# Taking every run-ending self-edge out of a graph layer's gathers, with the remaining edges stored end to end in DRAM

## The chip, the cores and the metric

The kernel runs on one core of one Trainium2 chip. The metric is the device time of one execution in microseconds. Before the change three runs took 15,846.22, 15,847.3 and 15,848.97 us; their median, 15,847.3, is the time that the prediction and the result are measured against. A profiled execution is a run of its own and takes a little longer than these.

## The reference

One layer of a graph network with 50,000 nodes and 1,650,000 edges. A node carries 160 numbers: 64 scalars `s` and 32 vectors `v` of three. Every edge takes the 160 numbers of its source node and four numbers of its own (`e0`, and a vector `e1`), makes a message of 160 numbers, and adds it to its destination node.

```python
loop = arange(50000)
src = concatenate([_s, _d, loop]); dst = concatenate([_d, _s, loop])
o = argsort(dst, stable=True); src = src[o]; dst = dst[o]
...
ss, vv = s[src], v[src]
dot = einsum('eui,ei->eu', vv, e1)
out0 = C0 * (ss * e0 @ W1 + dot * INV3 @ W2)
p3 = (ss @ W3)[:, :, None] * e1[:, None, :] * INV3
p4 = einsum('eui,uw->ewi', vv * e0[:, :, None], W4) * INV3
p5 = einsum('eui,uw->ewi', cross(vv, e1[:, None, :]), W5) * INV6
m = concatenate([out0, (C1 * (p3 + p4 + p5)).reshape(-1, 96)], axis=1)
m_agg = segment_sum(m, dst, num_segments=n)
h = concatenate([m_agg_s @ Ws * LIN_S, m_agg_v @ Wv * LIN_V])      # per node
out = layernorm(x + (x + relu(h)))
```

Three facts of it matter here. The edges come sorted by destination, 33 to a node in the mean, so those of one node are a run of neighbours. The list holds one self-edge for each node (source and destination are the same), and since the sort is stable, it is the last of its run; a random edge can be a self-edge too, but seldom. And the message is linear in the source's 160 numbers and in the edge's four, so the sum over edges of (attribute k times x of the source) can be formed first for each node and each of the four k, and the weights applied after it.

## The kernel before, in words

**Units, groups, pairs.** 128 edges are a *unit*, six units a *group* (768 edges), two groups a *pair*. A group's destinations lie in a window of W = 32 nodes that begins at the destination of the group's first edge. `gather` (L288) fetches the source rows of a unit by one indirect DMA of 128 rows of 640 bytes, which GpSimd issues (L292) with a column of the index tile `si`; a pair needs twelve, into one of six buffers `xg`. `spread` (L297) builds on VectorE, for the same pair, the matrix `ha`: for each unit, 128 edges by 4 x 32 columns, holding attribute k of the edge in column (k, node within the window). `group_sums` (L329) multiplies: for each unit a matrix product of `ha` (128 x 128) with the gathered rows (128 x 160), six units added up in PSUM (`ps`, two buffers). The result for a group is `A`, 4 x 32 rows of 160.

**Chunks and blocks.** Four groups are a *chunk*. `turn` (L459) transposes its `A`s on TensorE, `apply_weights` (L476) multiplies by the prepared weights BWa and BWb. A *block* is 128 nodes of the output, 391 in all. `nodes` (L493) loads the block's rows `xt` of x and builds `hot2`, which places the rows of some chunks in the block; `block` (L506) multiplies by it and, with `norm1` to `norm3`, adds x, normalizes, and the result is stored.

**Super-chunks.** Indices and attributes come in for 20 groups (ten pairs) at once: `load` (L235) reads them, `cast` makes floats of the source and destination numbers, `place` (L267) transposes them on TensorE, so that edges lie along the partitions, and writes `si`, the position in the window `rel`, and the attributes `pk`. Over the loop of pairs, the load of the next super-chunk is issued at the first pair of the present one, its cast a pair later and its place three pairs after that. The first position of each window, `baseB`, is read from the destinations once at the start.

**Self-edges taken out of rows.** The first 60 groups (three super-chunks, pairs 0 to 29) are taken from the edge list as it is. All later groups but the last few are cut from *rows* of 787 edges, out of which 19 self-edges are taken, so that 768 are left. 120 rows are a *pack*, one row on each of 120 partitions; there are 17. The generator `pack` (L354) does the work on VectorE: it reads sources, destinations and attributes of the rows (`prs`, `pra`), marks the self-edges, counts them by a running sum (`cum`), collects the four attributes of each (the accumulating products of L419, into `mine`), and closes the gaps by moves of 1, 2, 4, 8 and 16 places under a mask (L431 to L448). At the end three DMAs store the 120 x 768 edges left in DRAM (`sd`, `ad`; L454 and L455), which `load` reads back (L245, L246). What is taken out comes back in `own` and `group_sums`: SP loads for each packed group the 32 rows of x in its window, four times over (`xo`, 80 KB, at an address read into a register, L318 and L324), and VectorE adds `xo` times the taken attributes to `ps` (L343).

**Order.** Work is written out in the order of the pairs: `gather` of a pair, `spread` of the next one, the sums, and then a share of the steps of the pack in progress. The steps of a pack are spread evenly over the pairs until it is needed: the first pack over pairs 1 to about 18, each later one over the 60 pairs that use the pack before it (`when`). A scheduler then sets the final order of each engine's instructions; semaphores carry the dependences. All plain DMAs go through SP's queue, and each of them waits for the eighth DMA before it on that queue, since they share eight semaphores. The same holds for the gathers on GpSimd.

Of the kernel before, what the change touches and what calls it, by code (L numbers as in the profile page):

```python
# [25 lines left out]

# [7 lines left out]
F32 = mybir.dt.float32  # L35
# [29 lines left out]
RP = 120  # L65

# [3 lines left out]
def plan(n_nodes, n_edges):  # L70

    nblk = 125
    assert n_nodes % nblk == 0
    nb = n_nodes // nblk
    again = 9

    per_unit = P * n_nodes / n_edges
    group = max(g for g in range(1, 17)
                if g == 1 or (g + 0.2) * per_unit + 1 + 5 * math.sqrt(g * per_unit * per_unit / P) <= W)

    out = 0
    while out + 1 <= per_unit * group * (1 + 0.03) - 5 * math.sqrt(group * per_unit * per_unit / P + 1 / 6):
        out += 1
    row = group * P + out
    head = min(HEAD, math.ceil(n_edges / (group * P)))
    packed = max(0, (n_edges - head * group * P) // row // SG * SG) if out else 0
    rest = max(0, n_edges - head * group * P - packed * row)
    ngroups = head + packed + math.ceil(rest / (group * P))
    padded = QG * math.ceil(ngroups / QG)
    end = (head + padded - head - packed) * group * P + packed * row  # L90
    units = P * math.ceil(max(math.ceil(n_edges / P) + again - 1, math.ceil(end / P)) / P)
    return nblk, nb, again, group, units, ngroups, row, head, packed
# [3 lines left out]
def tile_gnn_resnorm(ctx: ExitStack, tc: tile.TileContext, x, src, dst, attr, W1, W2, W3, W4, W5, Ws, Wv, out, n_edges):  # L96
    nc = tc.nc
    N = x.shape[0]
    NBLK, NB, GA, G, NU, NG, L, NH, NPK = plan(N, n_edges)
    NCH = math.ceil(NG / QG)  # L100
    NGP = NCH * QG
    K = L - G * P

    def start(g):

        packed = min(max(g - NH, 0), NPK)
        return (g - packed) * G * P + packed * L

# [88 lines left out]
    def near(c):  # L197
        return start(c * QG) * N / n_edges

    step = QG * max(G * P, L) * N / n_edges  # L200
    off = 6 * math.sqrt(n_edges) / 2 * N / n_edges + W
# [10 lines left out]
    with tc.tile_pool(name="once", bufs=1) as once, tc.tile_pool(name="raw", bufs=2) as rawp, \  # L212
            tc.tile_pool(name="idx", bufs=2) as idxp, tc.tile_pool(name="rows", bufs=6) as rowp, \
            tc.tile_pool(name="far", bufs=3) as farp, tc.tile_pool(name="own", bufs=5) as ownp, \
            tc.tile_pool(name="pack", bufs=1) as packp, tc.tile_pool(name="self", bufs=2) as selfp, \
# [4 lines left out]
            tc.tile_pool(name="psM", bufs=2, space=PSUM) as psM:  # L220

        extremes = once.tile([P, 2, NSC], F32, name="extremes")
        baseB = once.tile([P, NGP], F32, name="baseB")
        rowid = once.tile([P, NCH], F32, name="rowid")
        bank = psC.tile([P, 3, P], F32, name="bank")
# [3 lines left out]

        own_eng = ET.Activation if ET.SP in HELP else ET.SP  # L230
        dq = nc.scalar if ET.SP in HELP else nc.sync
# [3 lines left out]
        def load(s):  # L235

            n = (min(NG, (s + 1) * SG) - s * SG) * G
            g0 = s * SG
            ra = rawp.tile([P, P, NK], F32, name="ra")
            if NH <= g0 < NH + NPK:  # L240
                sd, ad = stored[(g0 - NH) // RP]
                e = slice((g0 - NH) % RP * G * P, ((g0 - NH) % RP * G + n) * P)
                rf = rawp.tile([P, 2, P], F32, name="rf")
                for i in range(2):
                    dq.dma_start(rf[:n, i, :], sd[i:i + 1, e].rearrange("o (u p) -> (o u) p", p=P))  # L245
                dq.dma_start(ra[:n].rearrange("u p k -> u (p k)"), ad[e].rearrange("(u p) k -> u (p k)", p=P))  # L246
                return s, n, None, rf, ra
            e = slice(start(g0), start(g0) + n * P)
            ri = rawp.tile([P, 2, P], I32, name="ri")
            dq.dma_start(ri[:n, 0, :], src1[e].rearrange("(u p) o -> u (p o)", p=P))  # L250
            dq.dma_start(ri[:n, 1, :], dst1[e].rearrange("(u p) o -> u (p o)", p=P))
            dq.dma_start(ra[:n].rearrange("u p k -> u (p k)"), attr[e].rearrange("(u p) k -> u (p k)", p=P))
            return s, n, ri, None, ra

        def cast(loaded):
            s, n, ri, rf, ra = loaded
            if rf is None:
                rf = rawp.tile([P, 2, P], F32, name="rf")
                nc.scalar.copy(rf[:n], ri[:n])
            if HELP:  # L260

                ro = rawp.tile([P, P], I32, name="ro")
                nc.scalar.mul(ro[:n], rf[:n, 0, :], 4.0 * D)
                offsets[s] = ro
            return s, n, rf, ra

        def place(cast_):  # L267

            s, n, rf, ra = cast_
            pi = bank[:, 1:3, :]  # L270
            for i in range(2):
                nc.tensor.transpose(pi[:, i, :n], rf[:n, i, :], ident[:n, :n])
            pk = psK.tile([P, NK, P], F32, name="pk")
            for k in range(NK):
                nc.tensor.transpose(pk[:, k, :n], ra[:n, :, k], ident[:n, :n])
            si = idxp.tile([P, P], I32, name="si")
            nc.vector.tensor_copy(si[:, :n], pi[:, 0, :n])
# [4 lines left out]
                float(N - 1), baseB[:, s * SG:s * SG + n // G].unsqueeze(2).to_broadcast([P, n // G, G]),  # L282
# [26 lines left out]
        OWN = 5  # L309

        def own(p):

            s, g, ng = pairs[p]
            if not NH <= g < NH + NPK:
                return
            if p % OWN == 0:
                g1 = min(g + OWN * PG, NH + NPK)
                _, at = nc.values_load_multi_w_load_instructions(  # L318
                    baseO[0:1, g:g1], engines=[own_eng], min_val=0, max_val=(N - W) * 4 * D,
                    skip_runtime_bounds_check_because="an offset of a row of x")  # L320
                places.update(enumerate(at, g))
            xo = ownp.tile([P, PG, D], F32, name="xo")
            for i in range(ng):
                dq.dma_start(xo[:, i, :].bitcast(U8),  # L324
                             xbytes[ds(places.pop(g + i), W * 4 * D)].rearrange("(w f) -> w f", w=W).unsqueeze(0)
                             .to_broadcast([NK, W, 4 * D]))
            owns[p] = xo

        def group_sums(p, rows, ha):  # L329
# [7 lines left out]
            xo = owns.pop(p, None)  # L337
            if xo is None:
                evict(A[:, :ng], ps[:, :ng])
            else:  # L340
                for i in range(ng):
                    r = g0 - NH + i
                    nc.vector.scalar_tensor_tensor(A[:, i], xo[:, i], taken[r // RP][:, r % RP:r % RP + 1], ps[:, i],  # L343
                                                   op0=ALU.mult, op1=ALU.add)
            return A, ng

        owns, stored, taken, places = {}, {}, {}, {}
        halves = ((0, L // 2), (L // 2, L))

        degree = n_edges / N  # L350
        late = 6 * math.sqrt(L) + 2 * degree
        early = -6 * math.sqrt(L)

        def pack(c):  # L354

            r0 = c * RP
            n = min(RP, NPK - r0)
            e0 = start(NH + r0)
            e = slice(e0, e0 + n * L)
            prs = packp.tile([P, 2, L], F32, name="prs")  # L360
            pri = prs.bitcast(I32)
            pra = packp.tile([P, L, NK], F32, name="pra")
            pb = packp.tile([P, 1], I32, name="pb")
            dq.dma_start(pri[:n, 0, :], src1[e].rearrange("(r e) o -> r (e o)", e=L))
            dq.dma_start(pri[:n, 1, :], dst1[e].rearrange("(r e) o -> r (e o)", e=L))
            dq.dma_start(pra[:n].rearrange("r e k -> r (e k)"), attr[e].rearrange("(r e) k -> r (e k)", e=L))
            dq.dma_start(pb[:n], base_d[NH + r0:NH + r0 + n])
            yield
            for _ in range(3):
                yield  # L370
            nc.scalar.copy(prs[:n], pri[:n])
            yield
            marks = psP.tile([P, 512], F32, name="marks")
            m, mi = marks[:n], marks[:n].bitcast(I32)

            cum = packp.tile([P, L + 1], F32, name="cum")
            far = packp.tile([P, L], I32, name="far")
            less = packp.tile([P, L], I32, name="less")
            pbf = packp.tile([P, 2], F32, name="pbf")
            mine = packp.tile([P, 2, NK * W], F32, name="mine")  # L380
            waste = packp.tile([P, L], BF16, name="waste")
            nc.vector.tensor_scalar(pbf[:n, 0:1], pb[:n], float(N - W), None, op0=ALU.min)
            nc.vector.tensor_scalar(pbf[:n, 1:2], pbf[:n, 0:1], -1.0, None, op0=ALU.add)
            nc.vector.memset(mine, 0.0)
            nc.vector.memset(cum[:, 0:1], 0.0)

            for h, (a, e) in enumerate(halves):
                q = slice(0, e - a)
                col = slice(2 * c + h, 2 * c + h + 1)
                nc.scalar.copy(m[:, q], prs[:n, 1, a:e])  # L390
                nc.vector.tensor_tensor(m[:, q], prs[:n, 0, a:e], m[:, q], op=ALU.is_equal)
# [474 lines left out]
```

## Time and profile before

| | |
|---|---|
| three runs, median | 15,847.3 us |
| profiled execution | 15,876.85 us |
| its span | 15,875.1 us |
| granted TensorE clock, mean | 0.669 of full |
| TensorE matmul (PE) | 12,184.3 us busy, 77%, 43,039 instructions |
| TensorE weight load (PEld) | 8,889.9 us, 56% |
| VectorE (DVE) | 6,147.6 us, 39%, 14,632 |
| ScalarE (ACT) | 909.3 us, 6%, 2,081 |
| GpSimd (POOL) | 11,939.1 us, 75%, 12,606 |
| DMA | 1,386.00 MB, mean 87 GB/s |

The page gives for each engine the sum of its instructions' durations. A row of the costliest groups names the source line, the engine, the operation and its tiles (result, arrow, operands), then the count; behind the first bar busy time and the mean of one in ns, behind the second the idle time just ahead of these instructions and what ended it. A row of the timeline has the start in us from the beginning of the span, the busy time, the engine ("SPq" is the queue of DMAs that SP issues), line, operation, count, and in brackets how long the engine had been idle and what released it. "Issue" is idle time in which nothing is waited for that the profile shows. The last part of the page, the chain that ended last, covers less than 1% of this span, so the bound has to be found from groups and timelines.

### The profile page before, as it was taken

The page shows a single profiled execution, that of the slowest core. Times are in us where ns is not written, and L with a number is a line of the kernel's source. Part 1 is how long each engine was busy: PE and PEld are TensorE (multiplying, and loading weights), DVE is VectorE, ACT ScalarE, POOL GpSimd, SP SyncE. Part 2 cuts the span into 40 slices and gives each one's busy share as a digit, 9 for nine tenths or more (in the row PEclk, how much of TensorE's full clock was granted, in tenths as well). Part 3 has the DMA queues.
Part 4 walks back from the last instruction along what each step waited for, and adds up shares of the span by engine and source line. Part 5 has one row for each costly group of instructions (what it writes and reads, how often), then busy time and mean ns, then how long its engine had stood idle before and what let it go on. Part 6 is the DMA issues. An engine that isn't in the chain of part 4 may idle for free. (4 is left out here: it accounts for less than half of the span.)

```text
span 15875.1 us, 127140 instructions
## 1 busy us (share of the span) xinstructions
PE 12184.3 (77%) x43039; PEld 8889.9 (56%) x43040; DVE 6147.6 (39%) x14632; ACT 909.3 (6%) x2081; POOL 11939.1 (75%) x12606
## 2 busy tenths in 40 slices
PE   7677777777777777777777777777777777777777
PEld 5455555555555555555555555555555555555555
DVE  4543344443434343443434343433434343432222
ACT  0000000000000000000000000000000000000000
POOL 7777777777777777777777777777777777777776
PEclk6666666666666666666666666666666666666666
DMA  3333333333333333333333333333333333333332
GB/s 80 90 87 91 83 96 82 95 84 94 83 95 83 90 88 82 95 83 93 84 95 83 95 83 94 84 87 90 84 94 84 95 83 94 83 84 88 83 82 70
DMA packets 1045582, 1386.00 MB, mean 87 GB/s; under 512 B 233195, under 2 KB 818447, under 8 KB 1040753
## 3 DMA queue, kind: packets, MB, share of 16 engines
q0 software_dynamic: 604512, 1032.51, 27.0%
q1 hardware_dynamic: 439801, 344.75, 8.0%
q8 instruction: 338, 5.54, 0.2%
q14 instruction: 323, 2.65, 0.1%
q10 hardware_dynamic: 608, 0.55, 0.0%
HBM read 1307.42 MB, written 69.49 MB: 87 GB/s over the span
## 5 line engine op out<-in xcount | busy, mean ns | idle before, releaser
L292 POOL DMA_INDIRECT xg<-in_x,si x12594 | 11936.8, 948 | 3903.6 <-issue 3657.3
L334 PE MATMUL ps<-xg,ha 128*128 128x160 f32 x25188 | 8819.2, 457 | 3579.1 <-DMA xg<-in_x,si 3535.7
L334 PEld LDWEIGHTS ps<-xg,ha 128*128 128x128 f32 x25188 | 5613.2, 274 | 6208.0 <-DMA xg<-in_x,si 5628.7
L343 DVE SCALAR_TENSOR_TENSOR A<-xo,taken,ps 128x160 f32<-128x160 f32 x2020 | 682.1, 377 | 7006.9 <-PE ps L334 7003.6
L304 DVE TENSOR_TENSOR ha<-hot,pk 128x1536 f32<-128x1536 f32 x1050 | 1828.5, 1742 | 205.3 <-PE ps L334 205.3
L482 PE MATMUL phc<-BWb,at 32*128 32x160 f32 x4200 | 1610.1, 486 | 0.0
L419 DVE SCALAR_TENSOR_TENSOR waste<-marks,pra 120x236 bf16<-120x236 f32 (+45 forms) x2856 | 1492.2, 522 | 44.5
L512 PE MATMUL phb<-hp,hot 128*128 128x160 f32 x4538 | 1325.8, 395 | 0.3 <-DVE hot L502 0.2
L468 PE MATMUL pt<-ident,A 128*128 128x128 f32 (+1 forms) x4198 | 1292.2, 391 | 3.2 <-DVE A L343 0.9
L482 PEld LDWEIGHTS phc<-BWb,at 32*128 32x128 f32 x4200 | 919.3, 272 | 552.6 <-issue 552.6
L482 PE MATMUL phc<-BWa,at 128*128 128x160 f32 x4200 | 1149.4, 372 | 0.0
L512 PEld LDWEIGHTS phb<-hp,hot 128*128 128x128 f32 x4538 | 1082.1, 273 | 4.0 <-ACT at L471 3.5
L482 PEld LDWEIGHTS phc<-BWa,at 128*128 128x128 f32 x4200 | 919.5, 252 | 0.5 <-ACT at L471 0.2
L177 DVE SCALAR_TENSOR_TENSOR y<-phb,xt 128x160 f32<-128x160 f32 x391 | 125.8, 322 | 1969.8 <-PE phb L512 1969.1
L471 ACT COPY at<-pt 128x512 f32<-128x512 f32 (+1 forms) x1050 | 579.8, 579 | 4464.9 <-PE pt L468 4456.2
L468 PEld LDWEIGHTS pt<-ident,A 128*128 128x128 f32 (+1 forms) x4198 | 729.6, 176 | 87.6 <-DVE A L343 16.6
L301 DVE TENSOR_TENSOR hot<-bank,rel 128x384 f32<-128x384 f32 x1050 | 572.5, 546 | 2.4
L486 ACT COPY hp<-phc 128x160 f32<-128x160 f32 x525 | 153.6, 293 | 6019.0 <-PE phc L482 5982.1
L502 DVE TENSOR_TENSOR hot<-bank,rr 128x768 f32<-128x768 f32 (+2 forms) x391 | 357.9, 915 | 0.0
L186 ACT ACTIVATE rstd<-mv,eps_t 128x1 f32<-128x1 f32 x391 | 115.3, 295 | 3938.7 <-DVE mv L181 3902.5
L446 DVE COPY_PREDICATED pra<-marks,pra 120x1572 f32<-120x1572 int32 (+6 forms) x170 | 323.1, 1900 | 0.0
L419 DVE DVE_READ_ACCUMULATOR waste<-marks,pra 120x1 f32 (+1 forms) x2856 | 233.4, 82 | 0.0
(105 smaller groups left out, 1826.1 us busy)
## 6 DMA issues: line engine op xcount, KB each, us to landing
xg<-in_x,si POOLq DMA_INDIRECT x12594
xo<-in_x SPq DMA_DIRECT2D x2020, 80.0 KB
xt<-in_x SPq DMA_DIRECT2D x390, 80.0 KB
out<-o SPq DMA_DIRECT2D x390, 80.0 KB
ra<-ad SPq DMA_DIRECT2D x101, 240.0 KB
pra<-in_attr SPq DMA_DIRECT2D x16, 1475.6 KB
ad<-pra SPq DMA_DIRECT2D x16, 1440.0 KB
rf<-sd SPq DMA_DIRECT2D x202, 60.0 KB
```

What stands on the lines that cost most here:

```text
L292: nc.gpsimd.indirect_dma_start(out=xg[:, j, :], out_offset=None, in_=x, in_offset=bass.IndirectOffsetOnAxis(ap=placed[0][:, u + j:u + j + ...
L301: nc.vector.tensor_tensor(hot[:, :n], slotsP[:, 0:W].unsqueeze(1).to_broadcast([P, n, W]), rel[:, u:u + n].unsqueeze(2).to_broadcast([P, n ...
L304: nc.vector.tensor_tensor(ha[:, :n], hot[:, :n].unsqueeze(2).to_broadcast([P, n, NK, W]), pk[:, :, u:u + n].rearrange("p k u -> p u k").un ...
L334: nc.tensor.matmul(ps[:, j // G, :], ha[:, j].rearrange("p k w -> p (k w)"), xr, start=j % G == 0, stop=j % G == G - 1)
L343: nc.vector.scalar_tensor_tensor(A[:, i], xo[:, i], taken[r // RP][:, r % RP:r % RP + 1], ps[:, i], op0=ALU.mult, op1=ALU.add)
L419: nc.vector.scalar_tensor_tensor(waste[:n, w0:w1], m[:, w0 - a:w1 - a], float(w + 1), pra[:n, w0:w1, k], op0=ALU.is_equal, op1=ALU.mult, a ...
L446: nc.vector.copy_predicated(pra[:n, a:e], mi[:, r].unsqueeze(2).to_broadcast([n, e - a, NK]), pra[:n, a + d:e + d])
L468: nc.tensor.transpose(pt[:f1 - f0, g, :], A[:, i, f0:f1], ident)
L471: evict(at[:, :, :ng].rearrange("f k g w -> f g k w"), pt[:f1 - f0, :ng].rearrange("f g (k w) -> f g k w", w=W))
L482: nc.tensor.matmul(ph[:ng * W], at[:, k, :ng].rearrange("f g w -> f (g w)"), bw[:, k, :], start=i == 0, stop=i == 2 * NK - 1)
L502: nc.vector.tensor_tensor(hot2[:, :len(cs)], slotsP.unsqueeze(1).to_broadcast([P, len(cs), P]), rr[:, :len(cs)].unsqueeze(2).to_broadcast( ...
L512: nc.tensor.matmul(ph[:nb], hot2[:r, i, :nb], hp[:r], start=i == 0, stop=i == len(cs) - 1)
```

## The change

`plan` now counts with all self-edges that end a node's run, not with 19 in a row: a row is 790 edges, there are 2,033 rows in 17 packs, and what is left after the removal fills 2,086 groups instead of 2,099 (12,516 units in place of 12,594). How many edges are left of a row depends on the data, so rows can't be stored at fixed places. They are stored end to end in one DRAM array `edges`, six floats for each edge (source, destination, four attributes); each row's first position follows from its first destination, since one edge is taken for every node passed. `row_table` reads the first destination of all rows by one strided DMA and works out two tables of addresses, one for `edges` and one for the taken attributes, which go to an array `selves`, four floats for each node.

A row is stored by four DMAs, issued by SP, with addresses from registers that are loaded ten at a time (`store`, `put`): the row from its 33rd edge on (18,192 B), the first 32 edges (768 B), and two halves of the taken attributes (256 B each). All tails of a pack are stored first and all heads after them, so that a head overwrites what the row before it left beyond its own end. `load` reads a super-chunk by one DMA from `edges`, once all rows up to its end have been stored. In `pack`, source, destination and attributes stand together in `prow`, and one masked move serves all six. `place` works out the windows from the destinations that it has, by a product with ones on TensorE and some small operations.

The loads `xo` and VectorE's additions in `group_sums` leave; ScalarE copies `ps` to `A` for every pair, as it did for the first 60 groups. The self-edges' messages are added once a block: the new `own(b)` transposes the block's `xt`, multiplies by the weights for two k at a time, multiplies each by the node's taken attribute `sa` (loaded from `selves` in `nodes`) and adds; `block` adds the sum `t`. The gather buffers `xg` go from six to five. The steps of one pack at a time are spread over the pairs until its `due`.

```diff
-            tc.tile_pool(name="idx", bufs=2) as idxp, tc.tile_pool(name="rows", bufs=6) as rowp, \
+            tc.tile_pool(name="idx", bufs=2) as idxp, tc.tile_pool(name="rows", bufs=5) as rowp, \
...
         def load(s):
...
+            if g0 >= NH:
+                p0 = g0 * G * P - EH
+                r6 = rawp.tile([P, P, 2 + NK], F32, name="r6")
+                dq.dma_start(r6[:n].rearrange("u p c -> u (p c)"),
+                             edges[0, p0 * (2 + NK):(p0 + n * P) * (2 + NK)].rearrange("(u q) -> u q", u=n))
+                return s, n, None, r6[:n, :, 0], r6[:n, :, 1], r6[:n, :, 2:]
...
-            if NH <= g0 < NH + NPK:
-                sd, ad = stored[(g0 - NH) // RP]
...
         def place(cast_):
...
+            first = idxp.tile([P, SG], F32, name="first")
+            nc.vector.tensor_scalar(first[:n], starts[:n], df[:, 0:1], None, op0=ALU.mult)
+            nc.tensor.matmul(bank[:, 3, :ng], ones[:n], first[:n, :ng], start=True, stop=True)
+            gs = slice(s * SG, s * SG + ng)
+            nc.vector.tensor_scalar(baseB[:, gs], bank[:, 3, :ng], float(N - 1), None, op0=ALU.min)
...
-        def own(p):
...
             A = sump.tile([P, PG, D], F32, name="A")
-            xo = owns.pop(p, None)
-            if xo is None:
-                evict(A[:, :ng], ps[:, :ng])
-            else:
-                for i in range(ng):
-                    r = g0 - NH + i
-                    nc.vector.scalar_tensor_tensor(A[:, i], xo[:, i], taken[r // RP][:, r % RP:r % RP + 1], ps[:, i],
-                                                   op0=ALU.mult, op1=ALU.add)
+            evict(A[:, :ng], ps[:, :ng])
...
+        def row_table(tmp):
...
+                dq.dma_start(ti[:, :NR], dst[EH:EH + NR * L].rearrange("(o r e) -> o r e", o=1, e=L)[:, :, 0])
...
         def pack(c):
...
+            def begin():
+                T["rows"] = rows = packp.tile([P, L + 1, C], F32, name="prow")
+                nc.scalar.copy(rows[:n, :L, 0], T["pri"][:n, 0, :L])
+                nc.scalar.copy(rows[:n, :, 1], T["pri"][:n, 1, :])
+                nc.scalar.copy(rows[:n, :L, 2:], T["pra"][:n])
...
+                    nc.vector.copy_predicated(rows[:n, a:e], mi[:, r].unsqueeze(2).to_broadcast([n, e - a, C]),
+                                              rows[:n, a + d:e + d])
...
-            for i in range(2):
-                dq.dma_start(sd[i:i + 1].rearrange("o (r e) -> (o r) e", e=G * P), prs[:n, i, :G * P])
-            dq.dma_start(ad.rearrange("(r e) k -> r e k", e=G * P), pra[:n, :G * P])
...
+            def store(head, j):
...
+                _, at = nc.values_load_multi_w_load_instructions(
+                    row_at[0:1, i0:i0 + m], engines=[ET.SP], min_val=0, max_val=row_start(NR - 1)[0][1] * 4 * C,
+                    skip_runtime_bounds_check_because="held within bounds")
+                _, node = nc.values_load_multi_w_load_instructions(
+                    node_at[0:1, i0:i0 + m], engines=[ET.SP], min_val=0, max_val=row_start(NR - 1)[1][1] * 4 * NK,
+                    skip_runtime_bounds_check_because="held within bounds")
+                for i in range(m):
...
+                    e = slice(0, W) if head else slice(W, L)
+                    put(edge_bytes, v, e, C, T["rows"][p:p + 1, e, :])
+                    if r0 + p < real:
...
+                        e = slice(0, W // 2) if head else slice(W // 2, W)
+                        put(self_bytes, v, e, NK, T["mine"][p:p + 1, 0, e, :])
+
+            def put(mem, at, e, width, what):
+                size = (e.stop - e.start) * width * 4
+                dq.dma_start(mem[e.start * width * 4:][ds(at, size)].rearrange("(o f) -> o f", o=1),
+                             what.bitcast(U8).rearrange("p e c -> p (e c)"))
...
+            for head in (False, True):
+                steps += [partial(store, head, j) for j in range(RS)]
...
+            sa = np_.tile([P, NK], F32, name="sa")
+            dq.dma_start(sa[:nb], selves[0, row.start * NK:row.stop * NK].rearrange("(n k) -> n k", k=NK))
...
+        def own(b, xt, sa, hot2):
...
+                nc.tensor.transpose(pt[:f1 - f0, i, :nb], xt[:nb, f0:f1], ident[:nb, :nb])
+                evict(xT[:f1 - f0, i, :nb], pt[:f1 - f0, i, :nb])
+            t = np_.tile([P, D], F32, name="t")
+            for h in range(NK // 2):
+                y = psM.tile([P, 2, D], F32, name="yx", tag="misc")
+                ks = slice(2 * h, 2 * h + 2)
+                nc.tensor.matmul(y[:nb], xT[:, 0, :nb], BWa[:, ks, :], start=True, stop=False)
+                nc.tensor.matmul(y[:nb], xT[:D - P, 1, :nb], BWb[:, ks, :], start=False, stop=True)
...
+                        nc.vector.scalar_tensor_tensor(t[:nb], y[:nb, i], sa[:nb, k:k + 1], t[:nb],
+                                                       op0=ALU.mult, op1=ALU.add)
...
+            nc.vector.tensor_tensor(ph[:nb], ph[:nb], t[:nb], op=ALU.add)
             return norm1(np_, ph[:nb], xt[:nb], nb)
```

## The prediction

> **What bounds the kernel now.** I read the page's busy shares first, then its costliest groups, then GpSimd's timeline.
>
> ```profile
> PE 12184.3 (77%) x43039; PEld 8889.9 (56%) x43040; DVE 6147.6 (39%) x14632; ACT 909.3 (6%) x2081; POOL 11939.1 (75%) x12606
> ...
> L292 POOL DMA_INDIRECT xg<-in_x,si x12594 | 11936.8, 948 | 3903.6 <-issue 3657.3
> L334 PE MATMUL ps<-xg,ha 128*128 128x160 f32 x25188 | 8819.2, 457 | 3579.1 <-DMA xg<-in_x,si 3535.7
> ```
>
> ```profile
> 470.82 0.95 POOL L292 DMA_INDIRECT xg<-in_x,si  x1 [0.30 <-issue]
> 472.07 0.95 POOL L292 DMA_INDIRECT xg<-in_x,si  x1 [0.30 <-issue]
> 489.16 0.95 POOL L292 DMA_INDIRECT xg<-in_x,si  x1 [16.14 <-DVE si L277]
> ```
>
> GpSimd, not TensorE, sets the pace: TensorE's idle time is a wait for gathers, GpSimd's is almost only "issue". A gather takes 0.95 us and 0.30 of issue: one each 1.25 us, 15.02 us for a pair of groups (twelve). 12,594 x 1.2513 = 15,759 of the span's 15,875; the rest is the start (18.7), the end (33) and some 65 us of stalls. The largest stall, 16.1 us, is the third line: the first gather of pair 30, the first to use packed rows, waits for its indices. So there is little to win but gathers, and a lot to lose by anything that makes indices, or a free gather buffer, late.
>
> Why that stall exists is in the timelines of VectorE and of SP's queue:
>
> ```profile
> 370.46 1.75 DVE L304 TENSOR_TENSOR ha<-hot,pk 128x1536 f32<-128x1536 f32 x1 [6.10 <-PE ps L334]
> ...
> 464.46 1.81 DVE L446 COPY_PREDICATED pra<-marks,pra 120x1512 f32<-120x1512 int32 x1
> ```
>
> ```profile
> 464.19 1.20 SPq L454 DMA_DIRECT2D sd<-prs  x2
> 466.30 0.32 SPq L455 DMA_DIRECT2D ad<-pra  x1
> ...
> 476.68 0.81 SPq L245 DMA_DIRECT2D rf<-sd  x2
> ```
>
> VectorE ends the first block of rows only at 466 us, three DMAs store it, and the loads of super-chunk 3 follow. What comes between 466 us and those loads is on the path.
>
> **Prices on SP.** Per instruction, ns min/median/max:
>
> ```profile
> L324 SPq MOVE xo<-in_x x2020: 29/38/38, 39.1 to 15629.0; - x184
> L324 SPq DMA_DIRECT2D xo<-in_x x2020: 539/562/1667, 39.2 to 15629.0; - x184
> L318 SPq TENSOR_LOAD <-baseO x202: 1138/2244/2619, 37.9 to 15566.0; - x101
> L498 SPq DMA_DIRECT2D xt<-in_x x391: 328/359/495, 20.8 to 15835.6; - x196
> ```
>
> ```profile
> 6019.05 1.24 SPq L324 DMA_DIRECT2D xo<-in_x  x2
> ```
>
> A DMA at a fixed address holds SP for 0.36 us, one at an address from a register for 0.56, and two of these with a register move between them take 1.24, so 0.68 apart. A load of ten registers has two sizes in the trace (1.29 and 2.37) and a mean of 1.84.
>
> **What the Trainium skill says.** "DMA: Bandwidth & Descriptors", Rules for kernel authors: transfers under 64 KB are mostly overhead and should be coalesced. The stores added here are 18,192, 768 and 256 B; no run shows such a store yet. Same page, Anatomy of one DMA: about 2 us are fixed per DMA. The trace agrees: its semaphore events put an xt load's last increment 2.1 us (median) after its issue. Same page, Why a DMA increments its semaphore by 16 and not by 1: the number of DMA engines follows from the outermost dimension of the access, so a store from one partition may sit on one engine; no row of this trace is of that kind. "TensorE: Matmul & The Clock Gate", Part 1: activity releases the half clock. The trace fits: clock 0.67 while it waits for gathers.
>
> **The change, part by part.**
>
> *Gathers.* 2,086 groups instead of 2,099: 12,516 gathers, 78 fewer, x 1.2513 = 98 us gained. This part is certain; the built program holds that many.
>
> *Self messages.* Gone: 2,020 loads xo of 80 KB, 202 register loads on SP, 2,020 DVE adds (682 us). New: a copy of A on ACT for each pair (423 ns each in the 40 such copies of before, x 1,043 = 441 us; ACT is 6% busy), and for 391 blocks two transposes, four 320-column matmuls, four DVE products at about 0.38 us and an add at 0.32 (720 us of VectorE, 61% idle). TensorE: a 160-column pass advances 0.2 us at full, 0.37 at half clock in the timeline, so 4 to 7.4 us a block, 1.6 to 2.9 ms in all. Its 3.5 ms of waiting for gathers cover it, and more activity brings more full clock. I cost these at nothing; were TensorE's cover gone, the shortfall would be below 1 ms.
>
> *Start.* The first place now stands on VectorE behind two or three operations on a 1x2040 table, whose strided load comes first on SP: 10 to 15 us later, I take 12.
>
> *The stores.* Each block of 120 rows now leaves as one DMA per row for the tail (18,192 B), one for the head (768 B) and two of 256 B for the self attributes: 480 DMAs, almost all at addresses from registers, with 48 loads of ten registers. They replace three. In the built program the tails have one register operation each, the heads none, and every DMA waits for the one eight back, which at 2 to 4 us of landing is done by then. Price: 0.36 (fixed address) and 0.56 (128 rows from a register) bound one such DMA; a single row needs fewer descriptors, the address still comes from a register, so I take 0.48. With 0.045 of gap, and 0.075 more where there is a register operation: 0.60 for a tail, 0.525 for a head. Sum: 240 x 0.60 + 240 x 0.525 + 48 x (1.84 + 0.11) = 144 + 126 + 94 = 364 us. At the fixed-address price (0.48 and 0.405) it is 306, at xo's (0.68 and 0.60) 402.
>
> *First block.* VectorE: in the built order the product for pair 26 (370.5 in the timeline, plus 12) is followed by 84 collects where 37 stood, the messages of three blocks, then the shifts. The last message waits for TensorE's pair 25 (413), then 22 short collects, then 49 us of shifts (eight steps of 5.3, two of 3.4, as before: a 6-wide copy replaces a 4-wide and two): 413 + 3 + 20 + 49 + 12 = 497. All 480 stores are queued on SP ahead of the load for super-chunk 3: 497 + 364, and 9 for load, transposes and indices = 870. Gathers for pair 30 could start at 473 + 12 = 485. Stall 385 in place of 16: **+369**.
>
> *Later blocks.* 60 pairs apart. The last shift stands after the product for pair 113 (then 173, ...), which VectorE reaches 1 to 2 pairs ahead of its gathers, so stores start near pair 112.5. In 15 pairs (225 us) SP is given 369 us of work (5 for the xt, sa and out among them). Behind them wait the loads xt, the next super-chunk and, through the row buffer of which there is one, ACT's three copies of the next block, which stand after the copy of A for pair 129. ACT blocked there holds the two PSUM buffers, so the products of pair 132 stop, and with five gather buffers so does the gather of pair 137. That leaves 24.5 pairs = 368 us, less 13 (landing 2, ACT 5, TensorE 6): 355. Over by 14, and about 12 for xt and TensorE to catch up: 26 us, x 15 blocks = **+390**. The second block has 22 pairs: 369 - 317 + 12 = **+64**.
>
> Sum against the profiled execution (15,876.9; span 15,875.1): 15,877 - 98 + 12 + 369 + 64 + 390 = 16,614. The runs' median, 15,847.3, lies 30 lower: **16,580 us**.
>
> **Rivals.**
> *Cheap stores* (fixed-address price, 306 us for a block): the later blocks fit in 355 us and nothing stalls there; the first still does, by 327 - 16 = 311. 15,847 - 98 + 12 + 311 = 16,070. For it: a single row is less than xt's 128. Against it: xo's 0.2 us extra, which I lay on the register.
> *Dear stores* (xo's price, 402 us): first block +407, second +102, later (407 - 355 + 12) x 15 = 960: 17,230. The same lies near if all tails go through one DMA engine: in the burst of ad<-pra a 12,288 B packet took 0.72 us, so 18,192 B take up to 1.06, ten in each 16 us beside a gather's 0.34 each 1.25: 66% and 27%, near full. Gathers wait for the one eight back, 10 us; the trace shows 2.6 us of landing, and some 2 us of stall behind the 1.4 MB loads.
> *TensorE becomes the bound*, were its clock not released: some hundred us more, within the range.
> *Not slower*: the stores go out as fast as registers are moved. Then 98 - 12 = 86 us of gain must cover the first block, so 480 stores with their register loads must take under 81 us, 0.17 each. The register loads alone take 94 in the rows above, so this also needs them hidden behind VectorE's work; then 15,760.
>
> **From cases to numbers.** Likeliest case 0.40 (own range 16,350 to 16,850), cheap 0.25, dear or one DMA engine 0.25, TensorE 0.05, not slower 0.05. The ends are the two prices with their errors: 16,000 to 17,300. What a measurement here can tell from no change is 0.2%, 32 us: faster 0.03, same 0.02, slower 0.95.
>
> **What would show it.** 12,516 gathers at 1.25 us; one POOL stall of 300 to 430 us before pair 30, released by VectorE's si; on SP 8,128 DMAs of L540 with a median of 0.4 to 0.56 us; 15 stalls of equal size, 60 pairs apart, with ACT's copies waiting for stores. A first stall under 100 us would make it wrong, as would gathers of more than 1.25 us each away from stores, or a median under 0.2 us at L540.

## The result and the profile after

The changed kernel takes 16,056.3 us (median of four runs, 16,054.1 to 16,058.6), the kernel before 15,847.5 us in the same series: 208.8 us slower, ratio 1.0132 with a 95% interval of 1.0114 to 1.0149. The forecast was 16,580. The sign was right and the likeliest size was 3.5 times too large. The time lies closest to the rival *Cheap stores* (16,070), and so does the pattern: a stall at the first packed pair and nearly none later.

The page after, engines and costliest groups:

```profile
PE 12359.3 (77%) x47011; PEld 8724.9 (54%) x47012; DVE 6413.6 (40%) x15105; ACT 1574.3 (10%) x3873; POOL 11845.4 (74%) x12530
...
L302 POOL DMA_INDIRECT xg<-in_x,si x12516 | 11841.1, 946 | 4157.0 <-issue 3561.3
L324 PE MATMUL ps<-xg,ha 128*128 128x160 f32 x25032 | 7383.7, 423 | 3146.7 <-DMA xg<-in_x,si 3097.5
```

GpSimd still sets the pace: 12,516 gathers of 0.946 us with 0.30 us of "issue" each. What is new stands in GpSimd's timeline; the rows are starts, busy times, and in brackets the idle time before and its releaser:

```profile
486.08 0.94 POOL L302 DMA_INDIRECT xg<-in_x,si  x1 [0.30 <-issue]
775.38 0.94 POOL L302 DMA_INDIRECT xg<-in_x,si  x1 [288.36 <-DVE si L287]
```

```profile
1492.75 0.94 POOL L302 DMA_INDIRECT xg<-in_x,si  x1 [12.05 <-PE ptx L607]
```

These are all the stalls of more than 2 us beyond the usual 0.30: 288 us at the first packed pair (16 before) and 12 us at pair 77. After pair 100 no gap is 1.5 us longer than usual. Where the 288 us come from is in the timelines of VectorE and of SP's queue:

```profile
495.84 2.67 DVE L504 COPY_PREDICATED prow<-marks,prow 120x2274 f32<-120x2274 int32 x1
...
774.85 0.26 DVE L287 TENSOR_SCALAR si<-bank 128x120 int32<-128x120 f32 x1
```

```profile
763.14 0.23 SPq L540 DMA_DIRECT2D selves<-mine  x1
763.42 0.35 SPq L396 DMA_DIRECT2D pri<-in_dst  x1
763.83 0.40 SPq L398 DMA_DIRECT2D pri<-in_dst  x1
764.27 0.86 SPq L238 DMA_DIRECT2D r<-edges  x2
```

VectorE ends the rows of the first block at 498.5 us, SP has issued the 480 stores by 763.4, the load of super-chunk 3 follows at 764.3, and its indices are there at 775. And this is what a store and a register load cost SP (ns, min/median/max):

```profile
L540 SPq DMA_DIRECT2D edges<-prow x4066: 227/228/16622, 495.2 to 14889.8; - x194
L540 SPq DMA_DIRECT2D selves<-mine x4062: 227/228/325, 450.3 to 14890.1; - x194
```

```profile
L519 SPq TENSOR_LOAD <-ti x408: 957/1862/2773, 498.8 to 14880.1; - x136
```

A DMA of one row holds SP for 0.228 us, with 18,192 or 256 bytes alike, where the prediction took 0.48.

The whole difference, in the prediction's terms: 78 gathers fewer at 1.2513 us, -98; the stall at pair 30, 288.1 - 15.8 = +272; the stall at pair 77, +12; the first gather at 25.0 us instead of 18.7, +6; from the last gather to the end 50.3 us instead of 32.7, +18. Together +210, against 208.8 measured. (The two profiled executions differ by 177.2 us only, since that of before took 29 us more than its median and that of after 2 us less.)

### The profile page after: what moved, and what is told of

Same layout as the page of the kernel before. It is cut to its first block, busy times and chain, and to the rows that moved or that the text cites. A ratio compares the mean times of both kernels' runs of the same rounds, so it can differ in the third digit from the quotient of the medians.

```text
span 16052.3 us, 155475 instructions
## 1 busy us (share of the span) xinstructions
PE 12359.3 (77%) x47011; PEld 8724.9 (54%) x47012; DVE 6413.6 (40%) x15105; ACT 1574.3 (10%) x3873; POOL 11845.4 (74%) x12530
## 4 chain that ended last, share of the span: by engine, by line
POOL 46%; issue 21%; PE 16%; DMA 13%; SPq 3%; DVE 1%; ACT 0%; POOLq 0%; DVEq 0%; ACTq 0%
POOL xg L302 46%; DMA xg<-in_x,si 13%; PE ps L324 7%; PE yx L614 3%; PE yx L613 2%; SPq L540 2%; PE pt L559 2%; PE phb L630 1%; PE phc L573 1%; SPq L522 1%; SPq L519 1%; PE ptx L607 0%; DVE pra L465 0%; DVE prow L504 0%; PE pk L285 0%
## 5 line engine op out<-in xcount | busy, mean ns | idle before, releaser
L324 PE MATMUL ps<-xg,ha 128*128 128x160 f32 x25032 | 7383.7, 423 | 3146.7 <-DMA xg<-in_x,si 3097.5
L324 PEld LDWEIGHTS ps<-xg,ha 128*128 128x128 f32 x25032 | 4989.1, 254 | 5478.5 <-DMA xg<-in_x,si 4913.8
L465 DVE SCALAR_TENSOR_TENSOR pra<-marks,prow 120x236 bf16<-120x236 f32 (+40 forms) x2924 | 1501.6, 514 | 33.1
L327 ACT COPY A<-ps 128x320 f32<-128x320 f32 x1043 | 443.4, 425 | 6528.1 <-PE ps L324 6503.8
L614 PE MATMUL yx<-BWb,xT 32*128 32x320 f32 x1564 | 1000.3, 735 | 1.6 <-ACT xT L608 1.6
L613 PE MATMUL yx<-BWa,xT 128*128 128x320 f32 x1564 | 960.8, 713 | 0.7 <-ACT xT L608 0.7
L559 PE MATMUL pt<-ident,A 128*128 128x128 f32 (+1 forms) x4172 | 918.2, 371 | 42.8 <-DVE t L620 30.2
L630 PE MATMUL phb<-hp,hot 128*128 128x160 f32 x4688 | 892.6, 352 | 0.0
L573 PE MATMUL phc<-BWb,at 32*128 32x160 f32 x4176 | 771.4, 327 | 0.0
L620 DVE SCALAR_TENSOR_TENSOR t<-yx,sa,t 128x160 f32<-128x160 f32 x1173 | 445.0, 379 | 329.1 <-PE yx L614 323.3
```

The lines of the kernel that those rows point to most:

```text
L324: nc.tensor.matmul(ps[:, j // G, :], ha[:, j].rearrange("p k w -> p (k w)"), xr, start=j % G == 0, stop=j % G == G - 1)
L465: nc.vector.scalar_tensor_tensor(T["waste"][:n, w0:w1], T["marks"][:n, w0 - a:w1 - a], float(w + 1), T["rows"][:n, w0:w1, 2 + k], op0=ALU. ...
L559: nc.tensor.transpose(pt[:f1 - f0, g, :], A[:, i, f0:f1], ident)
L573: nc.tensor.matmul(ph[:ng * W], at[:, k, :ng].rearrange("f g w -> f (g w)"), bw[:, k, :], start=i == 0, stop=i == 2 * NK - 1)
L613: nc.tensor.matmul(y[:nb], xT[:, 0, :nb], BWa[:, ks, :], start=True, stop=False)
L614: nc.tensor.matmul(y[:nb], xT[:D - P, 1, :nb], BWb[:, ks, :], start=False, stop=True)
```

## The experiments

Two theories were set against each other first: that the loss is the first block alone, whose stores hold SP while no packed row is ready, and that it is spread over all blocks or over the new work in `own`. Then the price of a store and the limit of the later blocks were tried by themselves.

### More plain groups, 120 and 100 instead of 60

```diff
-HEAD = 60
+HEAD = 120
...
-    rows = math.ceil((n_edges - eh) / row) + 2
+    rows = math.ceil((n_edges - eh) / row) + 3
```

> First theory (the loss is the first block alone: its 480 stores hold SP for 265 us while no packed row is ready): with 120 plain groups instead of 60 the first packed pair is 60, not 30, the first block is due 30 pairs (450 us) later and its stores lie under gathers. Stall at pair 60 under 20 us; 12,528 gathers instead of 12,516, +15 us; 16,056 - 272 + 15 = 15,800, range 15,780 to 15,820. Rival (the loss is spread: own(b) on TensorE and the stores of all blocks slow the gathers): a few us at most are gained, 16,030 or more.

> 100 plain groups: first packed pair 50, 12,522 gathers (+7.5 us). First theory: the last masked move of the first block stands some 8 pairs ahead of the due pair 39, so stores run from pair 31 or 32 to pair 49 or 50 and super-chunk 5 is loaded right after: a stall of 5 to 60 us at pair 50; 15,795 to 15,850. Rival (spread loss): 16,030 or more.

In the first series of four kernels the one before took 19,139 us itself (11 runs, 19,088 to 19,225), and there this kernel took 20,782 us and the one with 100 groups 20,764. TensorE and SP were held up between instructions in the traces of that series: with 120 groups 2,643 us of TensorE's idle time are "issue", and none in the trace of the same kernel in the next series. So nothing is concluded from it; the same kernels ran again.

> The same kernel as e1_head120, since in the first call the kernel before itself took 19,139 us instead of 15,847: there TensorE and SP were held up between instructions, which says nothing on the two theories. With the kernel before near 15,847 us the expectation of e1_head120 stands: first theory 15,780 to 15,820 and no stall over 20 us at pair 60; rival 16,030 or more.

Measured: **15,749.9 us** (15,747.0 to 15,754.2) beside 15,845.9 for the kernel before; ratio 0.9940, interval 0.9926 to 0.9953. No stall at pair 60 or anywhere else over 2 us. Its gathers:

```profile
L302 POOL DMA_INDIRECT xg<-in_x,si x12528 | 11854.2, 946 | 3844.2 <-issue 3583.8
```

The stall of 288 us is gone for 12 gathers more, and so is the one of 12 us; this is 306 us less than the changed kernel and 96 less than the one before. The spread theory falls. The first block's rows are ready at 602.9 us, its stores issued by 874.0 (pair 56.2), and the first packed pair starts on time at 932.4. The result is 30 us below the range: the first stall went whole (288, not the 272 counted), and with it the second, 10 us at the start and the end, and some 10 us of gaps under 2 us.

> 100 plain groups, with the kernel before near 15,847 us: 12,522 gathers, 7.5 us fewer than with 120. With 120, stores ended at pair 56.2, 3.8 pairs before the first packed pair. With 100 they end between pair 47 and 50, super-chunk 5 is needed at pair 50: a stall of 0 to 30 us there, 15,742 to 15,775. Were the stores of the first block still exposed, some hundred us: 15,850 or more.

Measured: 15,846.9 us (12 runs), ratio 0.9999, interval 0.9991 to 1.0008. That misses the range by some 70 us and is what was named for stores still exposed:

```profile
883.06 0.94 POOL L302 DMA_INDIRECT xg<-in_x,si  x1 [97.18 <-DVE si L287]
```

The stores do not begin near pair 31 as expected. VectorE ends the first block's rows at 606.8 us (pair 38), as late as with 120 groups, and from there it takes 276 us to the first gather, as in the changed kernel (498.5 to 775.4: 277). Pair 50 was due at 786. What decides is the distance from the end of the moves to the first packed pair: it has to be 277 us. Why VectorE ends as late here as with 120 groups, though the block is due ten pairs earlier, is not shown.

### The kernel before with 80 plain groups

```diff
-HEAD = 60
+HEAD = 80
```

> The kernel before with 80 plain groups instead of 60, to part what the larger number gives by itself from what it gives to the change: the count of gathers stays 12,594, the first block of rows is needed ten pairs later, and the 16 us stall goes. 15,847 - 16 = 15,831, range 15,822 to 15,842.

Measured: 15,827.4 us, inside the range, ratio 0.9988, interval 0.9981 to 0.9994, and the first packed pair starts with no gap. So the larger number by itself is worth 20 us to the old kernel. The other 77 us of the best version (15,827.4 - 15,749.9) are the change's: 66 gathers fewer than 12,594 are 83 us at 1.2513.

### Stores to fixed addresses

```diff
-                _, at = nc.values_load_multi_w_load_instructions(
-                    row_at[0:1, i0:i0 + m], engines=[ET.SP], min_val=0, max_val=row_start(NR - 1)[0][1] * 4 * C,
...
+                    v = (r0 + p) * 766 * 4 * C
...
+                        v = (EH + (r0 + p) * L) // 33 * 4 * NK
...
-                dq.dma_start(mem[e.start * width * 4:][ds(at, size)].rearrange("(o f) -> o f", o=1),
+                dq.dma_start(mem[e.start * width * 4 + at:e.start * width * 4 + at + size].rearrange("(o f) -> o f", o=1),
```

> All 480 stores of a block go to fixed addresses, and the 48 register loads and the register moves are gone (rows then lie where they do not belong, so wrong edges are summed; the amount of work is the same). First theory: the DMA row stays at 0.23 us, with 0.07 between two that is 0.30 x 480 = 144 us for a block in place of 265; the stall at pair 30 falls from 288 to about 167, the one at pair 77 to nothing: 16,056 - 121 - 12 = 15,923. If a register address is what makes a DMA dearer, the row falls clearly below 0.23. Rival (VectorE's late end, not the stores, sets the stall): it stays within 20 us of 288.

> The same kernel as e3_fixed_addresses, with the kernel before near 15,847 us: a store at a fixed address with no register load. First theory: DMA row 0.23, pitch 0.30, 144 us a block; stall at pair 30 167 us instead of 288, at pair 77 none; 15,923, range 15,900 to 15,950. If the register is what costs, the DMA row falls well below 0.23 and the stall below 140. Rival (VectorE sets the stall): 288 within 20.

Measured, in one run each: 19,222 us in the first series, 15,948.3 later, 108 us less than with registers and inside the range. The row of one DMA and the first packed gather:

```profile
L532 SPq DMA_DIRECT2D edges<-prow x4066: 214/250/819, 502.2 to 14768.8; - x194
```

```profile
671.81 0.94 POOL L302 DMA_INDIRECT xg<-in_x,si  x1 [186.49 <-DVE si L287]
```

The stall falls from 288 to 186 us, though VectorE ends its rows 4 us later (502.2): it is SP's stores that fill it, and the theory that VectorE sets it falls. A DMA at a fixed address is not cheaper than one at a register's: 0.25 us against 0.228. What the registers cost are the loads (87 us in the first block of the changed kernel) and a move or two for each DMA. From the end of the moves the 395 stores that are left take 155 us (85 of the attributes' went out before), 0.39 each on average and not 0.30, so the stall is 19 us longer than forecast.

The packets in the trace show where that comes from. Heads and their attributes follow each other every 0.295 us, as forecast. Each tail is a single packet of 18,192 B that takes 0.68 us, no two of the 2,033 overlap, and the 120 of this block fill 83 of 84 us. SP is held through its wait for the DMA eight places back. For the whole run, and below it for the changed kernel (us in total, times, longest):

```profile
SPq L532 <- DMA edges<-prow: 981.5, 1745, 1.5
```

```profile
SPq L540 <- DMA edges<-prow: 41.2, 88, 1.2
```

With the register work between them the 120 tails of the first block hold 82 us of packets in 141 us, so there SP is seldom held.

### The loads xo at fixed addresses, in the kernel before

```diff
-                             xbytes[ds(places.pop(g + i), W * 4 * D)].rearrange("(w f) -> w f", w=W).unsqueeze(0)
+                             xbytes[23 * (g + i) * 4 * D:(23 * (g + i) + W) * 4 * D].rearrange("(w f) -> w f", w=W).unsqueeze(0)
```

> The kernel before, with the loads xo at fixed addresses near the right ones and no register loads (self-edges then take a wrong node's row in part of the groups; the same bytes and shapes are moved). The prediction laid the 0.20 us that an xo DMA costs over an xt DMA on the register. If so, the row falls from 0.56 to 0.36. The rival, after the stores with a register took 0.23: it is the shape (32 rows laid four times), and the row stays at 0.50 or more. The time: 15,847 within 15 either way, since SP is not on the path there.

Measured, in one run: 15,852.6 us, inside the range, and

```profile
L324 SPq DMA_DIRECT2D xo<-in_x x2020: 536/537/1698, 39.9 to 15604.6; - x184
```

It is 0.537 us without a register and 0.562 with one. Of the 0.20 us that an xo load costs over an xt load, 0.025 at most is the register's. By elimination the rest belongs to the shape, 32 rows laid four times over; another shape of that kind was not tried.

### All stores twice, and the stores of rows twice

```diff
                     put(edge_bytes, v, e, C, T["rows"][p:p + 1, e, :])
+                    dq.dma_start(spare[p:p + 1, e.start * C:e.stop * C], T["rows"][p:p + 1, e, :].rearrange("p e c -> p (e c)"))
...
                         put(self_bytes, v, e, NK, T["mine"][p:p + 1, 0, e, :])
+                        dq.dma_start(spare2[p:p + 1, e.start * NK:e.stop * NK], T["mine"][p:p + 1, 0, e, :].rearrange("p e k -> p (e k)"))
```

The second addition is left out where only rows are doubled.

> Each of the 480 stores of a block goes out a second time, to a spare array at a fixed address (nothing else is changed): 960 DMAs, 265 + 480 x 0.30 = 409 us of SP for a block. First theory with the prediction's budget of 355 us for a later block: stall at pair 30 288 + 144 = 432, at the second block 12 + 144 = 156, at each of 15 later ones 409 + 5 - 355 + 12 = 71: 16,056 + 144 + 144 + 1,065 = 17,410. Rival (later blocks have no such limit, SP's work there is hidden anyway): 16,056 + 144 and at most 144 at the second block, 16,200 to 16,345, and no stall over 5 us after pair 100.

> The same kernel as e4_stores_twice, for the same reason. With the kernel before near 15,847 us: first theory 17,410 with a stall of some 71 us at each later block; rival 16,200 to 16,345 and no stall over 5 us after pair 100.

> Only the 240 stores of rows (tails and heads) go out a second time, to a spare array at a fixed address; nothing else is changed. A later block then holds SP for some 421 - 72 = 349 us from its last masked move on (275 before, 421 with all stores twice). Theory of a budget (355 us by the prediction, 421 - 73 + 12 = 360 by the run with all stores twice): no stall, or under 5 us, at the 15 later blocks; first block 288 + 72 = 360, second 50 to 90: 16,056 + 72 + 40 to 80 = 16,168 to 16,210. Rival (every DMA more costs a share, with no threshold): half of what all stores twice cost at the later blocks, 37 x 15 = 550 us more: about 16,740.

Measured, in one run each: all twice 17,492.1 us (22,852 in the first series), 82 above the first theory and over a thousand above its rival; rows twice 16,895.9. GpSimd in the third block, all twice and rows twice:

```profile
2772.73 0.94 POOL L302 DMA_INDIRECT xg<-in_x,si  x1 [57.69 <-PE ps L324]
```

```profile
2640.55 0.94 POOL L302 DMA_INDIRECT xg<-in_x,si  x1 [44.19 <-PE ptx L609]
```

Both are the first gather of pair 137, the pair that the prediction named. The same stall returns at 197, 257 and so on, often with shorter ones two and four pairs earlier. Means of the third to the sixteenth block, from the end of the last masked move to the last store, with SP's other DMAs among them:

| | SP's stores, us | stall per block, us | stores less 343 us |
|---|---|---|---|
| the changed kernel | 276.5 | 0 | below 0 |
| rows twice | 388.7 | 44.6 | 45.7 |
| all twice | 421.5 | 78.4 | 78.5 |

343 comes from the prediction: a later block's stall is its stores less 355 us of room, plus 12 to catch up. Both runs over the limit fit that in the mean, and between them 33 us more of stores cost 34 us more of stall. Single blocks scatter (35 to 72 us with rows twice, 58 to 103 with all twice), and no run of this kind lies between 277 and 389 us, so whether the stall begins at 343 or with a jump at 355 is not shown.

Rows twice missed its number (16,190 for the theory) and lies nearer to the rival's 16,740: the 240 DMAs more took 112 us of SP, 0.47 each, not the 0.30 expected, so this run was over the limit too. Most of the excess is in the tails again: in the third block 240 of them, one packet at a time, take 230 us where 120 took 148. A rival without a limit would have one price for a microsecond of stores, but the first 112 us more cost 45 and the next 33 cost 34. Counted by DMAs (240 more cost 45 us, 480 cost 78) the means do not exclude it; for the limit speak the waits below, which end with the stores.

The way the stall takes is only in part the one predicted. In the third block with all stores twice, TensorE stops first, on the load xt that waits behind the stores on SP:

```profile
2751.74 0.48 PE L611 MATMUL ptx<-ident,xt 128*128 128x128 f32 x1 [87.19 <-DMA xt<-in_x]
```

In the same block with rows twice, ScalarE stops first, as predicted: behind the copy of A for pair 129, at its copy into the row buffer.

```profile
2609.90 2.91 ACT L406 COPY prow<-pra 120x3160 f32<-120x3160 f32 x1 [69.95 <-DMA spare<-prow]
```

TensorE stops 6 us after it, for xt again. Both waits end with the stores, and no run parts the one from the other.

### Without the self-edges' messages

```diff
         def own(b, xt, sa, hot2):
...
-                nc.tensor.matmul(y[:nb], xT[:, 0, :nb], BWa[:, ks, :], start=True, stop=False)
-                nc.tensor.matmul(y[:nb], xT[:D - P, 1, :nb], BWb[:, ks, :], start=False, stop=True)
...
+            return xt, sa, hot2
...
-            nc.vector.tensor_tensor(ph[:nb], ph[:nb], t[:nb], op=ALU.add)
```

> The changed kernel without own(b) and without the addition in block: the self-edges' messages are left out (transposes, four products and five VectorE operations for each of 391 blocks). The loads of xt and sa and all stores stay. First theory: TensorE's work there is covered; the stall at pair 30 stays at 288 within 10, the one at pair 77 (TensorE waiting for xt) goes, and the end is some 15 us shorter: 16,056 - 12 - 15 = 16,029, range 16,010 to 16,050. Rival (own(b)'s 1.96 ms of TensorE are on the path in part): below 15,950.

Measured, in one run: 16,051.2 us, a microsecond outside the range, 5 less than the changed kernel:

```profile
PE 11489.3 (72%) x43101; PEld 8546.1 (53%) x43102; DVE 5737.2 (36%) x13150; ACT 1393.9 (9%) x3091; POOL 11846.1 (74%) x12530
```

```profile
788.64 0.94 POOL L302 DMA_INDIRECT xg<-in_x,si  x1 [302.70 <-DVE si L287]
```

TensorE has 870 us less to do and VectorE 676, and no time comes of it: that work is covered. The end is 22 us shorter (last gather to end 27.9). The two stalls did not do as expected. The first is 14 us longer, not within 10 of 288, because VectorE ends the rows at 512.0 instead of 498.5: the order of its instructions is a different one here. The stall at pair 77 did not go but moved to pair 80, again 12 us, and is now a wait for the load of the next super-chunk behind the stores (stores end at 1541.8, the gather starts at 1552.5).

This run also bounds what the 343 us mean. In every second block from the fourth on, the last store leaves 362 us after the last masked move (58 to 91 us of it SP's wait for a result to send), and no gather is late. TensorE does not read xt here, and ScalarE's copies into the row buffer stand six pairs later in these blocks (in the fourth, behind the copy of A for pair 195, not 189). So the limit belongs to the order of the work that waits behind the stores, not to the stores.

## Why the prediction was right and wrong

**The bound and the gathers: right.** 12,516 gathers came at 1.25 us; nothing between stalls moved. Of the other signs named beforehand, the first stall (300 to 430 us) and the median of a store (0.4 to 0.56 us) came in lower, and the 15 equal stalls did not come.

**Self messages at nothing: right**, by the run without them. What the prediction left out is the end, where nothing covers `own` of the last blocks: 18 us.

**Start: half.** It is +6 us, not +12.

**The price of a store: the step that failed.** The prediction bounded a DMA by 0.36 us (fixed address, 128 rows) and 0.56 (address from a register), laid the difference on the register and took 0.48. Both bounds came from DMAs of another shape, and the value lies outside them: 0.228. The two runs at fixed addresses show that the register adds 0.025 us at most. The sum for the first block, 364 us, measured 265: 130 for the 480 DMAs with what follows each until the next instruction (0.27) instead of 252; 87 for the register loads (94); the rest, some 48, for moves and other register instructions, of which the prediction had counted 18.

**First block: right but for that term.** VectorE's end was put at 497 us and is 498.5; load, transposes and indices at 9 us and are 12. 497 + 265 + 9 less 485 is 286; the stall is 288.

**Later blocks: the limit fits, the side was wrong.** With stores of 364 us the prediction had 14 us too much, and with catching up 26 for each of 15 blocks. The stores took 276 us, so each block keeps 67 us of room and the whole term of 390 us is zero. That a small excess was multiplied by 15 made this the largest error of the sum, from the same 0.25 us in the price of a DMA. The mechanism was right in part. ScalarE's copies behind the row buffer were named as what stops TensorE; they do stop first in some blocks of the doubled runs, but TensorE's own wait for xt, which the prediction counted only as catching up, comes within 6 us of them or before them. That a sum made on ScalarE's path alone fits so well may be partly luck.

**Second block: too cheap in one respect.** +64 was forecast and 12 came, but the limit there is lower than the 305 us that follow from the prediction: 271 us of stores already cost 12 us. TensorE waits for xt ahead of that stall, 50 us and 22 us:

```profile
1428.39 0.47 PE L607 MATMUL ptx<-ident,xt 128*128 128x128 f32 x1 [50.21 <-DMA xt<-in_x]
...
1470.61 0.45 PE L607 MATMUL ptx<-ident,xt 128*128 128x128 f32 x1 [22.37 <-DMA xt<-in_x]
```

**The rivals.** *Cheap stores* had 0.25 and should have had most of the chance: its price, 306 us, was still too high, and what it left out (the end, the second block) made up for it, so its 16,070 is close partly by luck. *Dear stores* and *TensorE becomes the bound* did not come. One DMA engine for all tails did not come as a limit on the gathers: none was late by over 1.5 us in the 15 later bursts of stores. But the engine itself is in the traces: a tail is one packet of 0.68 us (the estimate was up to 1.06), no two overlap, and a store's semaphore is raised in two steps where an xt load's is raised in 16. With fixed addresses, and with rows twice, it is these packets that hold the tails. *Not slower* needed 480 stores in 81 us; even with no registers, 395 of them took 155.

## What to carry to other kernels

Many small stores at addresses from registers cost the issuing queue first: here 0.55 us each with all register work, a third of it for loading the registers. Close behind stood the one DMA engine that carries stores from one partition: without the register work a tail still took 0.69 us. Ask of each such burst what stands behind it on the same queue and when that is needed: the first burst, for which nothing had been prepared, cost 272 us, and the 15 like it, with 67 us to spare, cost nothing, so moving the first use away (306 us) was worth more than the cheaper stores that were tried (108). And bound an unknown DMA with a row of its own shape; where a small excess is multiplied by many blocks, say first on which side of the limit the price puts it.

## What the runs showed of the hardware

An address from a register adds 0.025 us at most to the time that a DMA holds SP's queue: 0.228 us with a register and 0.250 without for one row, 0.562 and 0.537 for 32 rows laid four times over. The bytes don't show there either: 18,192 and 256 B take the same 0.228 us. They show behind it: a store from one partition is one packet, 0.68 us for 18,192 B and 0.02 us for 256 B, and the tails go one after another as through a single DMA engine. A load of ten registers takes 0.96 to 2.77 us, 1.86 in the median.

Left open: which of the two waits behind the stores, TensorE's for xt or ScalarE's for the row buffer, would hold the gathers alone; and why in the first series SP and TensorE were held up between instructions (the kernel before 19,139 us, the best version 20,782), so that the kernel with more DMAs on SP was 8.6% slower there, and 0.6% faster in the next.
